# A two-layer vision tower on one core: queries of the first attention by pairs of chunks, its block work at other places, and the second layer's weights and first tokens loaded during the first layer

## The chip, the core and the metric

The kernel runs on 1 core of one Trainium2 chip. The metric is the device time in microseconds (us) of one execution. The engines are PE (TensorE, matrix multiplication), DVE (VectorE), ACT (ScalarE), POOL (GpSimd) and SP (SyncE, which here only issues DMAs). Everything is float32. Each engine takes its instructions in the order in which the program lists them and waits where an operand is not there yet.

## What is computed

An image tower for 128 images: a tokenizer (two convolutions) makes 64 tokens of 256 features for each image. Then come two layers, each one attention and one feed-forward part with experts. Cut to what matters here:

```python
h = tokenizer(x)                                   # (128, 64, 256)
# layer 0, attention over differences: no product of q and k, but relu(q - k)
Q, K, V = (layernorm(h) @ W.T for W in (Wq, Wk, Wv))          # 8 groups of 32 features
attn = einsum("bqkgd,d->bqkg", relu(Q[:, :, None] - K[:, None]), w_mlp) + b_mlp
attn = softmax(relu(attn), axis=2)
h = h + einsum("bqkg,bkdg->bqdg", attn, V)
# layer 0, four experts, each itself a small attention over 64-feature parts of a token
h = h + expert_mixture(layernorm(h))
# layer 1, linear attention: tokens at one position t of all 128 images form a row
h = h + linear_attention(layernorm(h))
# layer 1, eight experts, one for each token (routing by the largest gate, capacity 1280)
h = h + routed_experts(layernorm(h))
```

## The kernel before

The program is one sequence of five stages, and the order on every engine is the order in which the code lists the work (`tc.manual_schedule()`).

**First attention** (`relu_attention`, about 177 to 1080 us). The 128 images form 8 blocks of 16 images. A block's 64 query positions are done 8 at a time: 8 chunks in a block, 64 chunks in all, numbered n; I write j for n modulo 8, the place of a chunk within its block. Relu(q - k) of one chunk has 32 parts (16 pairs i of rows by 2 halves hf of the features). DVE makes 18 of these parts with `larger` (line 530: max(q, k), from which the key is taken off again by a sum made once for a block, `key_sums` and `correction`), POOL 12 with `difference` (line 538, finished by a Relu on ACT, line 539), and ACT alone the remaining 2 with `by_query` (line 548). PE then sums each part over the features with the weights `w_mlp` (`add`, line 340) into the PSUM tile `sc`. When a chunk is summed, the softmax of it is made during the next chunk: `less_max` (DVE, lines 564 to 566), `exponents` (ACT), `sums` (DVE), `weights` (POOL, line 578), `transpose` (PE, line 587), `transposed` (ACT).

A chunk's loop body (lines 703 to 759) is written out by hand. On PE its order is: `add(0,0)`, the place X, `add(8,0)`, `add(4,0)`, the queries of the next chunk (`queries`, line 459: 4 matmuls of 128 columns, which the trace shows as 8 records), the place Y, `add(8,1)`, `add(0,1)`, `add(4,1)`, the seeding of the next `sc` (line 523), the transposes of the last chunk's softmax (line 587), the place Z, `add(12,0)`, `add(12,1)`. On ACT the places O, A, B and C, on DVE V1 (after `less_max`) and V2 (late in the chunk), on POOL W (after `weights`) lie between the steps of the chunk.

The work of a whole block is put at these places by lines 632 to 690: for the next block the statistics and factors of its normalisation (V2, W), the normalised rows (A, B, C), their transposes (X, Z), the keys (`keys`, line 405, four half blocks), the values (`values`, line 424, four quarters), the key sums (Y); for the last block the product with the values (`outcome`, line 480), its transposes (`back`, line 498) and the sum into the stream h2 (`added`, DVE, line 508). Before the change the keys lie at X and Z of j = 4 and 5, the values at X of j = 6, X and Z of j = 7 and Y of the next j = 0; `added` lies once in j = 2, twice in j = 3 and once in j = 4.

The queries' PSUM tile `pc` holds one chunk, in a pool of two; 8 more columns of it take the row maximum of `less_max`.

**Expert attention** (`expert_attention`, to about 1864 us): 64 pairs of images, one after the other, each in a loop body (lines 1268 to 1306) with scores, softmax, product with the values, and `output` (line 1120), which adds the result to h2 in SBUF and after each fourth pair writes these four pairs to DRAM (`hd`, line 1127). The last pair's softmax, its transposes, `mixed` and `output` end the stage. Its softmax weights (`weights`, lines 1087 and 1088) are two POOL operations for each half.

**Linear attention** (`linear_attention`): it reads `hd` back by token position, 4 positions at a time for all 128 images (`Group.load`, line 1365). Before the first matmul it loads its weights on ACT's queue (lines 1335 to 1347), makes some constants on POOL, loads four groups, and runs for group 0: statistics (DVE, lines 1373 and 1374), factors (POOL, 1378 to 1381), normalisation (ACT, 1384), transposes (PE, 1393), queries and keys (PE, line 1421). The constants and small weights of the routing (`Routing.__init__`) are set up just ahead of it, on the same queues.

Routing and the routed experts follow; the change does not touch them.

Of the kernel before, what the change touches and what calls it, by code (L numbers as in the profile page):

```python
# [20 lines left out]
P = 128  # L21
# [269 lines left out]
class Shared:  # L291
# [3 lines left out]
    def __init__(self, c, ctx):  # L295
        def pool(name, bufs, **k):
            return ctx.enter_context(c.tc.tile_pool(name=name, bufs=bufs, **k))

        self.np_, self.bp = pool("an", 2), pool("ab", 2)
        self.atp, self.ep, self.small = pool("aat", 1), pool("ae", 2), pool("as", 1)  # L300
        self.psq = pool("apq", 4, space=PSUM)
# [5 lines left out]
def relu_attention(c, sh, wqkv, wmlp, bmlp, beside):  # L307
# [10 lines left out]
    with (  # L318
# [29 lines left out]
        class Block:  # L348
# [103 lines left out]
            def queries(self, q0):  # L452

                self.pc[q0] = pc = psc.tile([P, 2 * NB * 8 + 8], F32, tag="pc", name="pc")
                pq = pc[:, : 2 * NB * 8].rearrange("p (c i t) -> p c i t", c=2, i=NB)
                xi = self.xT.rearrange("p c n (b t) -> p c (n b) t", b=2)
                for fo in range(2):
                    for fi in range(2):
                        nc.tensor.matmul(  # L459
                            pq[:, fo],  # L460
                            w[:, fi, fo * P : (fo + 1) * P],
                            xi[:, fi, :, q0 : q0 + 8],
# [4 lines left out]
            def queried(self, q0):  # L467
                self.q[q0] = q = ep.tile([P, 2, NB // 2, 8], F32, tag="q", name="q")
                pq = self.pc[q0][:, : 2 * NB * 8].rearrange("p (c i t) -> p c i t", c=2, i=NB)
                nc.scalar.copy(q, pq[:, :, NB // 2 :])  # L470
# [39 lines left out]
        class Chunk:  # L510


            def __init__(self, blk, q0):
                self.blk, self.q0, self.parts, self.m = blk, q0, {}, {}
                self.pc = blk.pc.pop(q0)
                self.pq = self.pc[:, : 2 * NB * 8].rearrange("p (c i t) -> p c i t", c=2, i=NB)
# [43 lines left out]
            def less_max(self):  # L560
                self.e = e = ep.tile([P, 8, T], F32, tag="e", name="e")
                self.mx = mx = ep.tile([P, 8], F32, tag="mx", name="mx")
                pm = self.pc[:, 2 * NB * 8 :]
# [68 lines left out]
        for b, x in enumerate(blocks):  # L632
            n = 8 * b

            if b + 1 < len(blocks):
# [6 lines left out]
                for i in range(4):  # L642
                    at(n + 10 + i // 2, "XY"[i % 2], of(x.back, i))
                    at(n + 10 + (i + 1) // 2, ("V2", "V1")[i % 2], of(x.added, i))
# [15 lines left out]
            else:  # L660
                for i in range(NP):
                    at(n - 21 + i if b > 2 else 1 + i // 4, "V2", of(x.statistics, i))
                at(n - 17 if b > 2 else 2, "W", of(x.factors, 0, 4))
                at(n - 13, "W", of(x.factors, 4, 8))
# [11 lines left out]
            for fo in range(2):  # L676
                at(n - 4 + fo, "X", of(x.keys, 0, fo))
                at(n - 4 + fo, "A", of(x.keyed, 0, fo))
                at(n - 4 + fo, "Z", of(x.keys, 1, fo))
                at(n - 3 + fo, "O", of(x.keyed, 1, fo))  # L680
            at(n - 2, "X", of(x.values, 0))
            at(n - 2, "A", of(x.valued, 0))
            at(n - 2, "Y", x.key_sums)
            at(n - 1, "V1", x.correction)
            at(n - 1, "X", of(x.values, 1))
            at(n - 1, "A", of(x.valued, 1))
            at(n - 1, "Z", of(x.values, 2))
            at(n, "O", of(x.valued, 2))
            at(n, "Y", of(x.values, 3))
            at(n, "B", of(x.valued, 3))  # L690
# [8 lines left out]
        with tc.manual_schedule():  # L699
# [3 lines left out]
            for n in range(len(seq)):  # L703
# [18 lines left out]
                if n + 1 < len(seq):  # L722
                    seq[n + 1][0].queries(seq[n + 1][1])
# [41 lines left out]
def expert_attention(c, sh, hd, normw, wr, br, wqkv, wvT, wproj, bproj, wout):  # L765
# [227 lines left out]
    class Pair:  # L993
# [89 lines left out]
        def weights(self, x):  # L1083
# [3 lines left out]
            nc.gpsimd.tensor_mul(s2, s2, bcast(self.blk.gate[:, self.n, x::2], 1, 8))  # L1087
            nc.gpsimd.tensor_mul(e, e, bcast(sm, 2, T))  # L1088
# [31 lines left out]
        def output(self):  # L1120
# [5 lines left out]
            if p % 4 == 3:  # L1126
                nc.sync.dma_start(
                    hd[2 * p - 6 : 2 * p + 2].rearrange("(n b) t f -> (b t) n f", b=2),
                    h2[:, p - 3 : p + 1],
                )  # L1130

# [82 lines left out]
    def first(cur, new, chunk, last):  # L1214
# [39 lines left out]
        last.added(3)  # L1254
        for k in range(NB):
# [4 lines left out]
    def rest(chunk, last):  # L1260
        with (
# [6 lines left out]
            for p in range(NP):  # L1268
                new = Pair(p + 1, blocks[(p + 1) // NB]) if p + 1 < NP else None
                if p == 0:  # L1270
                    first(cur, new, chunk, last)
                    old, cur = cur, new
                    continue
                do((p, "ACT"))
# [12 lines left out]
                cur.exponents(0)  # L1287
                if new:
# [8 lines left out]
                cur.weights(1)  # L1297
                do((p, "POOL"))
                old.mixed()
                if new:  # L1300
                    for h in range(2):
                        new.values(h)
                        new.values_kept(h)
                old.output()
# [11 lines left out]
def linear_attention(c, hd, hx, out, k, wqk, bqk, wv, bv, wgb):  # L1316
# [7 lines left out]
    NG = 4  # L1324
    with (
        tc.tile_pool(name="lw", bufs=1) as wp,
# [932 lines left out]
```

## Time and profile before

| | us |
|---|---|
| median of 3 runs | 2670.72 (2669.07 to 2671.12) |
| the profiled execution, its own time | 2667.24 |
| span of that execution in the profile | 2665.5 |
| PE busy | 2523.5 (95%) |
| DVE busy | 2009.8 (75%) |
| POOL busy | 1627.9 (61%) |
| ACT busy | 1621.5 (61%) |

The span runs from the first to the last instruction. Busy time is the union of the engine's instructions, averaged over five stages with different limits, so that a share of the whole span says little about one stage. The granted TensorE clock is 0.983 of full speed over the span and 1.00 in the first attention. In the trace a float32 matmul of the code shows as two records.

### The profile page before, as it was taken

To read this page: it belongs to the slowest core of one execution; us is meant where nothing else is said; L and a number is where in the kernel's file an instruction comes from. 1 tells how busy PE (TensorE), PEld (TensorE's weight loads), DVE (VectorE), ACT (ScalarE), POOL (GpSimd) and SP (SyncE) were. 2 spreads that over 40 slices of the span, in tenths; PEclk is the share of its full clock that TensorE was granted. 3 is DMA by queue.
4 is the path that set the end of the run, shared out by engine and by line. 5 is a ranking of instruction groups with operands and counts; after the bars stand their busy time and mean duration, and the time that the engine had idled before them with its cause. 6 is when DMAs were issued, how large, how long until landed. Compare 5 with 4: busy or idle time off the path is not lost.

```text
span 2665.5 us, 81705 instructions
## 1 busy us (share of the span) xinstructions
PE 2523.5 (95%) x35613; PEld 1729.0 (65%) x35613; DVE 2009.8 (75%) x2998; ACT 1621.5 (61%) x3421; POOL 1627.9 (61%) x1426
## 2 busy tenths in 40 slices
PE   8989999999999999899999999998899987999997
PEld 4554444444444444688888888887466565888886
DVE  5759999999999999778787878776467786444443
ACT  2228889898898988666666666665344533232332
POOL 3319999999899999565666665643233313444544
PEclk9999999999999999999999999999899998999998
DMA  3000000000000000000000000000434454555554
GB/s 112 33 13 1 2 1 2 1 2 2 1 2 1 2 13 2 3 20 11 12 19 12 11 20 12 19 12 17 121 73 110 95 127 151 190 183 200 190 186 134
DMA packets 138274, 141.19 MB, mean 53 GB/s; under 512 B 107875, under 2 KB 121701, under 8 KB 130224
## 3 DMA queue, kind: packets, MB, share of 16 engines
q1 hardware_dynamic: 127536, 118.40, 14.7%
q0 software_dynamic: 7648, 14.77, 1.8%
q8 instruction: 281, 4.60, 0.7%
q10 hardware_dynamic: 2720, 2.69, 0.3%
q14 instruction: 89, 0.73, 0.1%
HBM read 104.03 MB, written 32.54 MB: 51 GB/s over the span
## 4 chain that ended last, share of the span: by engine, by line
PE 75%; DVE 13%; issue 5%; ACT 4%; POOL 2%; DMA 1%; SPq 0%; POOLq 0%; DVEq 0%; ACTq 0%
PE sc L340 15%; PE po L2103 6%; PE ph L2087 6%; PE pc L184 5%; PE pt L1097 4%; PE sc L1061 4%; PE pqk L1014 4%; PE pq L1421 4%; PE pv L1036 3%; PE pz L1110 3%; PE pt L587 2%; DVE m L530 2%; PE pc L459 2%; PE pk L405 2%; DVE mx L1073 2%
## 5 line engine op out<-in xcount | busy, mean ns | idle before, releaser
L538 POOL TENSOR_TENSOR m<-q,k 128x1024 f32<-128x1024 f32 x384 | 719.7, 1907 | 56.4 <-PE sc L340 44.5
L530 DVE TENSOR_TENSOR m<-pc,k 128x2048 f32<-128x2048 f32 (+1 forms) x320 | 646.4, 2056 | 0.5 <-ACT q L470 0.5
L340 PE MATMUL sc<-m,wide 128*32 128x512 f32 x4096 | 517.1, 597 | 8.5 <-ACT m L539 6.2
L539 ACT ACTIVATE m<-m 128x1024 f32<-128x1024 f32 x384 | 403.1, 1051 | 21.3 <-POOL m L538 21.3
L340 PEld LDWEIGHTS sc<-m,wide 128*32 128x32 f32 x4096 | 130.9, 109 | 270.1 <-issue 159.4
L548 ACT ACTIVATE m<-k,q 128x64 f32<-128x64 f32 x1024 | 271.1, 340 | 0.9 <-DVE k L417 0.9
L1073 DVE TENSOR_REDUCE mx<-sc 128x16 f32<-128x1024 f32 x128 | 156.0, 1219 | 135.3 <-PE sc L1061 135.3
L1088 POOL TENSOR_TENSOR e<-e,mx 128x1024 f32<-128x1024 f32 x128 | 243.5, 1902 | 10.1 <-POOL mx L1087 0.2
L1020 ACT COPY kr<-pqk 128x512 f32<-128x512 f32 x254 | 137.9, 604 | 142.1 <-PE pqk L1014 142.1
L2087 PE MATMUL ph<-xt,w1s 128*128 128x256 f32 x896 | 198.7, 379 | 3.4 <-DVE xt L2078 2.7
L1087 POOL TENSOR_TENSOR mx<-mx,gate 128x16 f32<-128x16 f32 x128 | 27.6, 216 | 280.3 <-ACT z L1118 150.9
L2103 PE MATMUL po<-w2s,hT 128*128 128x256 f32 x896 | 198.0, 379 | 0.0
L2087 PEld LDWEIGHTS ph<-xt,w1s 128*128 128x128 f32 x896 | 169.9, 190 | 27.9 <-DVE xt L2078 3.4
L2103 PEld LDWEIGHTS po<-w2s,hT 128*128 128x128 f32 x896 | 168.1, 190 | 21.7
L1100 ACT COPY pT<-pt 128x512 f32<-128x512 f32 x256 | 139.0, 600 | 51.6 <-PE pt L1097 51.4
L1074 DVE TENSOR_TENSOR e<-sc,mx 128x1024 f32<-128x1024 f32 x128 | 156.7, 1224 | 4.4
L2121 POOL DMA_INDIRECT out<-y,rout x56 | 56.7, 1013 | 167.8 <-ACT hT L2091 124.8
L1080 DVE TENSOR_REDUCE mx<-e 128x16 f32<-128x1024 f32 x128 | 152.5, 1191 | 4.6 <-ACT e L1077 4.5
L1097 PE MATMUL pt<-ident,e 128*128 128x128 f32 x1024 | 143.0, 282 | 10.0 <-DVE vr L1050 7.3
L2091 ACT ACTIVATE hT<-ph,w1s 128x256 f32<-128x256 f32 x224 | 93.0, 470 | 96.9 <-PE ph L2087 96.9
L2108 ACT ACTIVATE y<-y,gf 128x256 f32<-128x256 f32 x56 | 28.0, 507 | 196.0 <-issue 107.3
L1077 ACT ACTIVATE e<-e 128x1024 f32<-128x1024 f32 x128 | 139.6, 1090 | 1.6 <-DVE e L1074 1.6
(331 smaller groups left out, 5009.6 us busy)
## 6 DMA issues: line engine op xcount, KB each, us to landing
w1s<-in_we SPq DMA_DIRECT2D x30, 1028.0 KB, 5.1
w2s<-in_we SPq DMA_DIRECT2D x30, 1024.0 KB, 4.8
hd<-h SPq DMA_DIRECT2D x16, 512.0 KB, 3.2
x<-hd SPq DMA_DIRECT2D x16, 512.0 KB, 3.6
h<-hd SPq DMA_DIRECT2D x4, 2048.0 KB, 12.7
hx<-h SPq DMA_DIRECT2D x4, 2048.0 KB, 11.7
out<-h SPq DMA_DIRECT2D x4, 2048.0 KB, 20.5
xt<-in_x SPq DMA_DIRECT2D x15, 512.0 KB, 3.5
```

What stands on the lines that cost most here:

```text
L340: nc.tensor.matmul(dst[j : j + 32], wide[:, hf, s : s + 32], part, start=start, stop=stop)
L530: nc.vector.tensor_tensor(m, bcast(self.pq[:, hf, i : i + n], 3, T), k, ALU.max)
L538: nc.gpsimd.tensor_tensor(m, bcast(self.q[:, hf, s : s + 2], 3, T), k, ALU.subtract)
L539: nc.scalar.activation(m, m, AF.Relu)
L548: nc.scalar.activation(self.parts[i, hf][:, q], self.blk.k[:, hf, i], AF.Relu, bias=self.q[:, hf, i - NB // 2, q : q + 1], scale=-1.0,)
L1073: nc.vector.tensor_reduce(mx, sc, AX.X, ALU.max)
L1074: nc.vector.tensor_sub(e, sc, bcast(mx, 2, T))
L1080: nc.vector.tensor_reduce(self.sm[x], self.e[x], AX.X, ALU.add)
L1088: nc.gpsimd.tensor_mul(e, e, bcast(sm, 2, T))
L1097: nc.tensor.transpose(pt[:, cq, :], e[:, i : i + 2, :].rearrange("p e s -> p (e s)"), c.ident)
L2087: nc.tensor.matmul(ph[:, j], self.w1[:, w0 : w0 + P], self.xt[:, fc], start=(fc == 0), stop=(fc == 1))
L2103: nc.tensor.matmul(po, self.hT[:, f, r * P : r * P + P], self.w2[:, f, :], start=(f == 0), stop=(f == 7))
```

## The change

Items 1 and 2 are in the first attention, item 3 is a layout of SBUF that item 4, at the border to the second layer, needs.

1. `queries` makes the queries of two chunks at once: one PSUM tile `pc` holds both, and each matmul has 256 columns instead of 128. The calls come in the chunks j = 0 (for the chunks 2 and 3), j = 3 (4 and 5), j = 5 (6 and 7) and j = 7 (0 and 1 of the next block). The row maximum of `less_max` goes into a part of the chunk's own queries that is no longer needed.
2. The block work lies at other places. Keys: Y and Z of j = 4 and 5, the copies at B and O. Values: Y of j = 2, 4, 6 and 7, copies at B. `added`: twice in j = 2 and twice in j = 3. The factors on POOL: from j = 7 and j = 3 to j = 1 and j = 6.
3. The pools of the tiles `at`, `e`, `q` go to the right side of SBUF, so that they can be closed after the first pair of the expert attention. Their room then holds the new class `Front`.
4. `Front` loads the linear attention's weights at pair 8 of the expert attention on SP's queue, and the first 16 token positions (four groups) as rows of images, one piece each time four pairs have been written, the last two images straight from h2 in SBUF. The last three pairs are written to `hd` in pieces of 2, 1 and 1 pairs. In the last pair `mixed` and `output` of the pair before it come ahead of the softmax sums, three matmuls without use follow them on PE, and the second half's weights are made on DVE. The linear attention starts with seven matmuls without use, normalises group 0 in two halves of two positions, and puts the routing's loads behind group 4's load and its constants into the first head's loop.

```diff
-                self.pc[q0] = pc = psc.tile([P, 2 * NB * 8 + 8], F32, tag="pc", name="pc")
-                pq = pc[:, : 2 * NB * 8].rearrange("p (c i t) -> p c i t", c=2, i=NB)
-                xi = self.xT.rearrange("p c n (b t) -> p c (n b) t", b=2)
+                pc = psc.tile([P, 2, 2, NB, 8], F32, tag="pc", name="pc")
+                for k in range(2):
+                    self.pc[q0 + 8 * k] = pc[:, k]
+                xi = self.xT.rearrange("p c n (b s k t) -> p c s k (n b) t", b=2, k=2, t=8)
                 for fo in range(2):
                     for fi in range(2):
                         nc.tensor.matmul(
-                            pq[:, fo],
+                            pc[:, :, fo],
                             w[:, fi, fo * P : (fo + 1) * P],
-                            xi[:, fi, :, q0 : q0 + 8],
+                            xi[:, fi, q0 // 16],
...
-                pm = self.pc[:, 2 * NB * 8 :]
+                pm = self.pq[:, 0, 0]
...
-                    at(n + 10 + (i + 1) // 2, ("V2", "V1")[i % 2], of(x.added, i))
+                    at(n + 10 + i // 2, ("V1", "V2")[i % 2], of(x.added, i))
...
-                at(n - 17 if b > 2 else 2, "W", of(x.factors, 0, 4))
-                at(n - 13, "W", of(x.factors, 4, 8))
+                at(n - 15 if b > 2 else 2, "W", of(x.factors, 0, 4))
+                at(n - 10, "W", of(x.factors, 4, 8))
...
-                at(n - 4 + fo, "X", of(x.keys, 0, fo))
-                at(n - 4 + fo, "A", of(x.keyed, 0, fo))
+                at(n - 4 + fo, "Y", of(x.keys, 0, fo))
+                at(n - 4 + fo, "B", of(x.keyed, 0, fo))
...
-            at(n - 2, "X", of(x.values, 0))
-            at(n - 2, "A", of(x.valued, 0))
             at(n - 2, "Y", x.key_sums)
             at(n - 1, "V1", x.correction)
-            at(n - 1, "X", of(x.values, 1))
-            at(n - 1, "A", of(x.valued, 1))
-            at(n - 1, "Z", of(x.values, 2))
-            at(n, "O", of(x.valued, 2))
-            at(n, "Y", of(x.values, 3))
-            at(n, "B", of(x.valued, 3))
+            for i, k in enumerate((6 - (b == 1), 4, 2, 1)):
+                at(n - k, "Y", of(x.values, i))
+                at(n - k, "B", of(x.valued, i))
...
-                if n + 1 < len(seq):
-                    seq[n + 1][0].queries(seq[n + 1][1])
+                two = {0: 2, 3: 1, 5: 1, 7: 1}.get(n % 8)
+                if two and n + two < len(seq):
+                    x, q0 = seq[n + two]
+                    x.queries(q0)
...
+            if p == NP - 1:
+                front.rows(B - 2, B)
+            n = {NP - 3: 2, NP - 2: 1, NP - 1: 1}.get(p, 4 * (p % 4 == 3))
+            if n:
                 nc.sync.dma_start(
-                    hd[2 * p - 6 : 2 * p + 2].rearrange("(n b) t f -> (b t) n f", b=2),
-                    h2[:, p - 3 : p + 1],
+                    hd[2 * (p - n + 1) : 2 * p + 2].rearrange("(n b) t f -> (b t) n f", b=2),
+                    h2[:, p - n + 1 : p + 1],
                 )
+            if p == NP - 3:
+                front.rows(B - 16, B - 8)
+            elif p == NP - 2:
+                front.rows(B - 8, B - 2)
+            elif n == 4 and p > 3:
+                front.rows(2 * p - 14, 2 * p - 6)
...
+                if p == 8:
+                    front.weights()
...
                 cur.exponents(0)
+                if not new:
+                    old.mixed()
+                    old.output()
+                    c.busy(ps([P, 2 * D], "idle"), wt.w, 3)
...
-                cur.weights(1)
+                cur.weights(1, nc.gpsimd if new else nc.vector)
...
+    def rows(self, b0, b1):
+        nc, NG = self.c.nc, self.NG
+        n = 4 * NG
+        x = self.x.rearrange("p g t f -> p (g t) f")
+        if b1 < B:
+            nc.sync.dma_start(x[b0:b1], self.hd[b0:b1, 0:n, :])
+            return
+        for b in range(2):
+            nc.sync.dma_start(x[b0 + b : b0 + b + 1], self.c.h2[b * T : b * T + n, B // 2 - 1, :])
...
         with tc.manual_schedule():
+            c.busy(psp.tile([P, 2 * D], F32, tag="pp", name="idle"), w[:, 0], 7)
             for g in range(4):
-                groups[g].load()
+                groups[g].x = front.group(g)
             for g in range(3):
                 for i in range(NG):
                     groups[g].statistics(i)
-                groups[g].factors()
+                    if g == 0 and i % 2:
+                        groups[0].factors(i - 1, i + 1)
+                        for j in range(i - 1, i + 1):
+                            groups[0].normal(j)
                 if g == 0:
-                    for i in range(NG):
-                        groups[0].normal(i)
                     groups[0].transpose()
+                else:
+                    groups[g].factors()
             groups[4].load()
+            routing.load()
...
+        at(0, 9, routing.constants)
+        at(0, 10, lambda: routing.weights_sum(psp.tile([P, 2 * D], F32, tag="pp", name="pw")[:, 0:E]))
```

## The prediction, made before the changed kernel had run

> **What bounds the kernel now.** I read the page first, then the windows of one steady block of the first attention (chunks 24 to 31), then the timeline of a chunk, and last the timeline at the border of the layers.
>
> ```profile
> PE 2523.5 (95%) x35613; PEld 1729.0 (65%) x35613; DVE 2009.8 (75%) x2998; ACT 1621.5 (61%) x3421; POOL 1627.9 (61%) x1426
> PE 75%; DVE 13%; issue 5%; ACT 4%; POOL 2%; DMA 1%; SPq 0%; POOLq 0%; DVEq 0%; ACTq 0%
> ```
>
> The chain that ends last is PE for three quarters. The change can pay where PE is too late, or where nobody works. The eight chunks of a block, in order j = 0 to 7 (stretch, its length, then busy time of PE, weight loads, DVE, ACT, POOL):
>
> ```profile
> 533.60:546.80 13.20, 13.20 (x132) 6.21 (x128) 12.72 (x12) 11.96 (x28) 12.29 (x8) 1.00 0.01 1
> 546.80:560.00 13.20, 13.20 (x372) 6.66 (x368) 12.77 (x13) 11.81 (x28) 12.32 (x8) 1.00 0.02 4
> 560.00:573.60 13.60, 13.38 (x128) 5.74 (x124) 13.29 (x13) 13.24 (x33) 12.20 (x8) 1.00 0.01 2
> 573.60:587.70 14.10, 14.10 (x132) 5.98 (x124) 13.87 (x15) 12.21 (x29) 13.09 (x11) 1.00 0.00 1
> 587.70:602.10 14.40, 14.40 (x118) 5.49 (x120) 13.32 (x15) 13.49 (x33) 13.11 (x9) 1.00 0.00 1
> 602.10:616.40 14.30, 14.30 (x124) 6.12 (x120) 12.71 (x13) 12.40 (x29) 12.24 (x8) 1.00 0.01 2
> 616.40:629.20 12.80, 12.80 (x160) 6.37 (x156) 12.59 (x12) 10.53 (x24) 12.28 (x8) 1.00 0.00 1
> 629.20:643.70 14.50, 14.50 (x132) 7.27 (x128) 12.96 (x15) 13.27 (x34) 13.84 (x12) 1.00 0.01 2
> ```
>
> PE looks full everywhere, but that is the modelled end of a matmul. DVE is nearly as full: 104.2 of 110.1 us. So two limits alternate: DVE binds where its busy time is within 0.3 us of the length (j = 2, 3, 6), PE where DVE has a gap of 0.4 to 1.6 us. What PE needs I took from the timeline, from a group's start to the next group's start:
>
> ```profile
> 602.76 1.98 PE L405 MATMUL pk<-xT,w 128*128 128x512 f32 x4
> 606.53 1.16 PE L459 MATMUL pc<-xT,w 128*128 128x128 f32 x8
> 617.08 1.99 PE L424 MATMUL pv<-w,xT 128*128 128x256 f32 x8
> ```
>
> Half a block of keys holds PE 1.91 us, the queries of a chunk 1.09, a quarter of the values 1.92 (1.82 right behind other full matmuls). In the same way: the 32 sums of a chunk 7.0, seeding 0.97, softmax transposes 1.08, half an outcome 1.41, four transposes 0.55 to 0.59, key sums 0.5. At the border:
>
> ```profile
> 1857.14 1.97 PE L1097 MATMUL pt<-ident,e 128*128 128x128 f32 x8 [0.19 <-POOL e L1088]
> 1863.30 0.42 DVE L1125 TENSOR_TENSOR h<-h,po 128x256 f32<-128x256 f32 x1 [8.50 <-PE po L1124]
> 1863.75 0.36 SPq L1127 DMA_DIRECT2D hd<-h  x1
> ...
> 1874.73 0.43 DVE L1373 BATCH_NORM_STATS2 st<-x 128x6 f32<-128x256 f32 x1 [0.68 <-DMA x<-hd]
> ...
> 1879.08 2.07 ACT L1384 ACTIVATE x<-x,nb,rs 128x256 f32<-128x256 f32 x4 [17.00 <-DVE mv L1374]
> ...
> 1882.36 7.88 PE L1421 MATMUL pq<-w,xT 128*128 128x512 f32 x16
> ```
>
> From the end of the last addition (1863.72) to the first product of the second layer (1882.36) PE has nothing of use for 18.64 us: 2.9 for the write to DRAM, about 1 of restart, 7.0 for the read back, 7.6 for statistics, factors, normalisation and transposes.
>
> **What the Trainium skill says.** "TensorE: Matmul & The Clock Gate", section "LDWEIGHTS (loading the stationary operand)": a weight load takes the time of its columns, whatever its number of rows. The trace agrees: 8 loads for the queries take 0.97 us, 0.12 each, as much as their 128 columns of data, so that 256 columns behind one load use it better. The same page, "What's actually happening": after an idle window of about 3.4 us the array runs at half clock until it has been busy as long. The trace fits: the 8 transposes of the last pair take 1.97 us, those inside the loop 1.09. "DMA: Bandwidth & Descriptors", section "Latency and other measured facts", speaks of a fixed cost of about 2 us for one DMA; here the write of 512 KB lands 2.9 us after its issue, so a small copy can't land much before 2.
>
> **The change, part by part.**
>
> *Queries by two.* Removed: eight times 1.09 a block. Added: four times 1.92 (8 records of 128 columns by 256, the form of the values' row). On PE 8.7 - 7.7 = 1.0 us less a block.
>
> *Keys and values at Y.* Nothing is added or removed, but a stretch of full matmuls that stands alone costs about 0.2 us more than one behind another (1.92 against 1.82, and the split of the sums), and four X places fall away: 0.1 to 0.2 each. With that, PE's need by chunk (sums, seeding, transposes 9.05, plus block work) is, before: 13.1, 13.0, 11.9, 11.9, 14.0, 14.0, 12.6, 14.0. After: j = 0 12.2; j = 1 11.9; j = 2 12.6 (values come in); j = 3 12.6; j = 4 14.6 (9.05 + keys 1.91 + values 1.82 + keys 1.91 - 0.1); j = 5 14.6 (9.05 + queries 1.92 + keys 1.8 + 1.9); j = 6 11.4; j = 7 12.6.
>
> *Additions.* Each `added` costs DVE 0.6 (0.68 busy, overlapped). One moves from j = 4 to j = 2. DVE's need with its small gaps (the busy column plus 0.25) becomes: 12.95, 12.95, 14.25, 14.1, 12.9, 12.95, 12.85, 13.15.
>
> The time of a chunk is the larger need, with 0.1 for PE-bound ones: 12.95 + 12.95 + 14.25 + 14.1 + 14.7 + 14.7 + 12.85 + 13.15 = 109.65 against 110.1. Gains are in j = 7 (14.5 to 13.15) and 0 and 1 (0.25 each), losses in j = 2, 4 and 5. So almost all that PE gains is stopped by DVE. I take 0.5 to 1.0 a block, since the 0.25 is generous where DVE is ahead: 5.5 for seven blocks. The first query call lies on the path and becomes 0.85 longer (chunk 0 was made in 0.89); net 5. Bounds: a loss of 6, if each of j = 4 and 5 also costs the 0.4 below, and a gain of 15, if DVE's own sum were nearly reached.
>
> *What waits with it.* The key and value copies move on ACT from A to B; an ACT that is there before PE has done Y stands with `by_query` and the Relus behind it, and PE waits for these. In j = 4 ACT reaches B some 5.0 us after the chunk's last sum (5.65 at 607.72 less the copies that left), values are ready at 5.7: 0.4 to 0.7 late, against a wait of 0.76 that ACT has anyway later in this chunk (before the `transposed` copy). I cost it at nothing.
>
> *Factors on POOL.* 1.7 us (four operations) more in j = 1 and 6 instead of 3 and 7. POOL stands 0.8 to 2.0 us for PE in most chunks, which hides most; the rest is caught up in the longer j = 2 and 7. Nothing. *Pools moved to the right side*: no instruction.
>
> *Last pair.* The second half's weights on DVE: about 0.2 + 1.22 instead of 0.22 + 1.90 on POOL behind the first half. But the sums now stand behind `added` of pair 62, which waits for its product (about 1852.3 instead of sums from 1851.15): some 1.5 late. The two cancel (1857.1 either way). The three unused matmuls keep the clock: transposes 1.09 for 1.97, `mixed` 2.1 for 2.56. Gain 0.7; between -0.8 and +1.5.
>
> *First tokens.* All rows but the last two images' are in SBUF before the end (96 KB follow the write of pair 62, nine us ahead). After the last addition two copies of 16 KB from h2: two issues of 0.36 on SP and 2.0 to 2.9 to land, so the statistics begin 2.5 to 3.3 after the addition instead of 11.0. From there: two positions' statistics 1.1, factors 1.9 on POOL, twice in a row (the second pair's end 5.0 after landing), normalisation 1.1, last transpose and copy 1.2: 7.2 to 7.4 against 7.6. The first product comes at +10.3 instead of +18.64: gain 8.3; between 7.5 and 9. SP has the last write to hd behind the two copies, then group 4, which waits for the transposes of group 0 as before. The seven unused matmuls (7 x 0.86 = 6 us) end before the transposes.
>
> *Weights and constants.* Seven DMAs on an SP queue that has one write in four pairs, five memsets of 0.2 on POOL at pair 8: hidden by POOL's idle time, 0 to 0.5. The routing's weight sum, hidden in the gap before, now lies between products: +0.5.
>
> Sum: -5 - 0.7 - 8.3 + 0.5 = -13.5. On the profiled execution: 2667.2 - 13.5 = 2653.7. That execution was 3.5 us below the median, so the median becomes 2670.7 - 13.5 = 2657.
>
> **The rivals.**
>
> *DVE takes it all*: the attention stays as it is, the border pays 9.0 less 0.5 and the 0.85 of the first queries: 2663. For it: DVE's 104.2 of 110.1. Against: j = 7 and 0 are clearly PE's.
>
> *The stalls go too*: PE's and DVE's limits no longer alternate, and a block nears DVE's sum plus its gaps, 106: seven times 4, and 8.5: 2634 to 2642, say 2638. Against it: `less_max` waits for the last sum of each chunk, so that neither engine can run more than a part of a chunk ahead.
>
> *Tokens don't come early*: SP works in order, the last rows wait for the write of pair 62, and a copy into a single partition may be slow. If the statistics start as before, 5 + 0.7 remain: 2665.
>
> *Slower*: the full stretch of 3.7 us at Y in j = 4, 5 and 7, with the copies at B. If ACT stands there for the whole last step (1.9) and only its 0.76 of slack hides it, each of the three chunks grows by about 1.2: 3.6 x 7 = 25 us, the 5 are not won, the border gives 8.5 back: 2687. It decides once ACT's wait at B exceeds some 0.8 us in these chunks.
>
> **How the numbers follow.** Forecast 2657 with 0.54, DVE takes it all 0.22, stalls gone 0.08, tokens late 0.08, slower 0.08. The range from 2645 to 2668 holds the forecast with its bounds and two rivals, and leaves out the far gain and the far loss. What a measurement can tell from no change is 0.2%, 5.3 us: faster means below 2665.4. Of the forecast nearly all is below, of the DVE case three quarters, of the late tokens half, all of the far gain: 0.81. Slower than 2676 is the last case and a rest, 0.08; 0.11 lies between.
>
> **What would show it.** In the changed profile a steady block near 109 to 109.6, with j = 4 and 5 at 14.7 and j = 7 near 13.1, DVE at 104 as before; the queries' rows 8 records of 128x256 in about 2.0; from the last addition to the first product about 10 us; the last transposes near 1.1. It is wrong if ACT's key or value copies show waits over 0.8 us, if j = 4 or 5 pass 15, or if the statistics of group 0 begin more than 4 us after the last addition.

## The result, and the profile after

The changed kernel takes 2805.66 us (median; 2797.19 to 2808.93), the kernel before, run beside it, 2669.89. The ratio is 1.0508, with a 95% interval from 1.0493 to 1.0523: 5% slower, 136 us, where 2657 had been forecast. The profiled execution has a span of 2806.1 us against 2665.5.

From the page of the changed kernel, the engines and then five groups (busy time, mean of one in ns, idle time of the engine ahead of them, and what ended most of it):

```profile
PE 2576.6 (92%) x35377; PEld 1720.8 (61%) x35377; DVE 2017.0 (72%) x3000; ACT 1625.6 (58%) x3421; POOL 1628.5 (58%) x1428
...
L540 POOL TENSOR_TENSOR m<-q,k 128x1024 f32<-128x1024 f32 x384 | 720.1, 1907 | 74.6 <-PE sc L342 60.4
L532 DVE TENSOR_TENSOR m<-pc,k 128x2048 f32<-128x2048 f32 (+1 forms) x320 | 646.8, 2057 | 124.1 <-ACT q L473 124.1
L342 PE MATMUL sc<-m,wide 128*32 128x512 f32 x4096 | 552.8, 616 | 106.6 <-DVE m L532 96.3
L541 ACT ACTIVATE m<-m 128x1024 f32<-128x1024 f32 x384 | 399.9, 1049 | 109.8 <-POOL m L540 109.8
...
L581 POOL TENSOR_TENSOR e<-e,mx 128x512 f32<-128x512 f32 x64 | 66.9, 1045 | 149.5 <-DVE mx L578 119.8
```

Three of these groups on the page of the kernel before, where their lines have other numbers:

```profile
L530 DVE TENSOR_TENSOR m<-pc,k 128x2048 f32<-128x2048 f32 (+1 forms) x320 | 646.4, 2056 | 0.5 <-ACT q L470 0.5
L340 PE MATMUL sc<-m,wide 128*32 128x512 f32 x4096 | 517.1, 597 | 8.5 <-ACT m L539 6.2
L539 ACT ACTIVATE m<-m 128x1024 f32<-128x1024 f32 x384 | 403.1, 1051 | 21.3 <-POOL m L538 21.3
```

The busy times of DVE, POOL and ACT are nearly those of before (DVE 2017.0 against 2009.8). PE's is 53 us longer, but it has 236 instructions fewer; its sums took longer one by one (616 ns on average, 597 before). So no work has been added. The new thing is on the right. `larger` on DVE had 0.5 us of idle time ahead of it and now has 124.1, all ended by line 473, ACT's copy of the queries (`queried`). The sums on PE wait 106.6 instead of 8.5, the Relus on ACT 109.8 instead of 21.3, the weights on POOL 149.5 instead of 21.9. The timeline below shows how the one stall is handed on to these. The list of waits (total, times, longest) counts it:

```profile
PEld sc L342 <- DVE m L532: 167.3, 96, 2.8
...
DVE m L532 <- ACT q L473: 124.1, 32, 4.7
POOL e L581 <- DVE mx L578: 119.8, 37, 6.6
```

DVE waits 32 times, once in every second chunk, 3.9 us on average.

To place it I measured each chunk from the start of one row maximum (`less_max`) to the next. Chunks 24 to 31 of the changed kernel, j = 0 to 7 (stretch, length, then busy time and instructions of PE, weight loads, DVE, ACT, POOL, then the granted clock):

```profile
585.20:603.07 17.87, 14.53 (x159) 5.58 (x153) 12.82 (x12) 13.38 (x33) 13.19 (x8) 1.00 0.00 1
603.07:616.03 12.96, 12.90 (x358) 6.38 (x337) 12.74 (x13) 11.04 (x25) 11.62 (x11) 1.00 0.02 4
616.03:634.38 18.35, 15.31 (x134) 6.05 (x128) 14.01 (x14) 14.83 (x35) 14.80 (x10) 1.00 0.00 1
634.38:648.43 14.05, 13.88 (x124) 5.98 (x124) 13.84 (x14) 12.16 (x29) 12.08 (x7) 1.00 0.01 1
648.43:666.01 17.58, 14.99 (x116) 5.69 (x116) 12.81 (x13) 12.89 (x30) 11.28 (x8) 1.00 0.00 1
666.01:680.73 14.72, 14.72 (x124) 6.26 (x120) 12.72 (x12) 12.44 (x29) 12.26 (x8) 1.00 0.01 2
680.73:699.15 18.42, 15.08 (x152) 6.47 (x148) 12.82 (x13) 10.73 (x24) 13.97 (x12) 0.81 0.00 1
699.15:713.19 14.04, 13.76 (x124) 6.20 (x120) 12.91 (x13) 11.77 (x27) 12.29 (x8) 1.00 0.01 2
```

The even chunks take 17.6 to 18.4 us, where before they took 12.8 to 14.4; the odd ones are at 12.96 to 14.72. DVE's busy time in the even ones is what it was, but for the `added` that moved from j = 4 to j = 2. The last chunk's clock is an average; the last section comes back to it. From the first row maximum to the last the stage takes 1010.3 us instead of 864.6: 145.7 more, while everything else together takes 5.1 less.

Inside one even chunk (j = 4; start, length, engine and line, and in brackets the idle time ahead of it and who ended it):

```profile
648.43 0.69 DVE L567 TENSOR_REDUCE pc<-sc 128x8 f32<-128x512 f32 x1
...
649.42 0.69 DVE L569 SCALAR_TENSOR_TENSOR e<-sc,mx 128x512 f32<-128x512 f32 x1
...
650.15 0.63 ACT L574 ACTIVATE e<-e 128x512 f32<-128x512 f32 x1 [1.26 <-DVE e L569]
650.68 1.05 ACT L550 ACTIVATE m<-k,q 128x64 f32<-128x64 f32 x4
...
651.64 1.99 ACT L541 ACTIVATE m<-m 128x1024 f32<-128x1024 f32 x2
...
653.53 0.24 ACT L473 COPY q<-pc 128x128 f32<-128x128 f32 x1
...
653.81 2.29 DVE L532 TENSOR_TENSOR m<-pc,k 128x2048 f32<-128x2048 f32 x1 [3.69 <-ACT q L473]
...
656.02 0.68 DVE L577 TENSOR_REDUCE mx<-e 128x8 f32<-128x512 f32 x1
...
656.15 1.06 PE L342 MATMUL sc<-m,wide 128*32 128x512 f32 x8 [0.67 <-DVE m L532]
...
657.10 1.04 POOL L581 TENSOR_TENSOR e<-e,mx 128x512 f32<-128x512 f32 x1 [4.83 <-ACT m L541]
...
659.14 1.06 PE L342 MATMUL sc<-m,wide 128*32 128x512 f32 x8 [1.92 <-DVE m L532]
...
660.04 1.06 ACT L541 ACTIVATE m<-m 128x1024 f32<-128x1024 f32 x1 [2.06 <-POOL m L540]
```

After the row maximum and the exponent's argument (until 650.1) DVE's next instruction is `larger(0,4,1)`. It reads this chunk's columns of the query tile and the keys, and both have long been there. It starts only at 653.81, just after ACT has copied out the queries of the *other* chunk of the pair (653.53 + 0.24). ACT gets to that copy late, since the exponentials, a `by_query` step of four instructions and two Relus stand before it in its queue. From there the stall runs on: DVE's softmax sums come late, so POOL stands 4.83 before the weights (the bracket names ACT, but over the program the list of waits puts most of this on DVE's sums, 119.8), so POOL's next differences and ACT's Relus are late (2.06), and PE waits for DVE's parts (0.67 and 1.92). Before, the same two instructions lay side by side:

```profile
648.32 3.37 DVE L530 TENSOR_TENSOR m<-pc,k 128x2048 f32<-128x2048 f32 x2
...
649.27 0.24 ACT L470 COPY q<-pc 128x128 f32<-128x128 f32 x1
```

There the copy (for the next chunk) ran in the middle of two of DVE's maxima. It read another PSUM tile, since each chunk had its own. Over the whole trace, 63 of the 64 copies overlapped one of DVE's maxima in time. In the changed kernel 31 of the 32 copies from the next pair's tile still do, but none of the 32 from the tile that DVE is reading.

So the change made a wait that no line of it names: two chunks' queries lie in one PSUM tile (512 columns), DVE reads one half, ACT the other, and DVE's read is ordered behind ACT's. The order stands in the program as built: in the trace `larger(0,4,1)` waits on ACT's semaphore in all 32 even chunks and in no odd one, and in none of the 64 chunks before the change. The Trainium skill, "PSUM — Partial Sum Buffer", section "PSUM bank collisions raise a hardware error ⚠️", says that two engines must not be in one bank and quadrant at once, and that the compiler's scheduler "adds a dependency between any two instructions on different engines that touch the same bank × 32-partition quadrant, reads and writes alike". The trace agrees that two reads by two engines were ordered, in 32 waits of up to 4.7 us. Whether this rule or the sharing of the tile as such put the order into the program, the runs can't separate.

The border of the layers, in the changed kernel:

```profile
2008.34 1.09 PE L1098 MATMUL pt<-ident,e 128*128 128x128 f32 x8 [0.20 <-DVE e L1089]
...
2013.64 0.42 DVE L1126 TENSOR_TENSOR h<-h,po 128x256 f32<-128x256 f32 x1 [5.36 <-PE po L1125]
2014.09 1.25 SPq L1389 DMA_DIRECT2D x<-h  x2
...
2017.08 0.43 DVE L1429 BATCH_NORM_STATS2 st<-x 128x6 f32<-128x256 f32 x1 [3.02 <-DMA x<-h]
...
2019.98 1.09 ACT L1441 ACTIVATE x<-x,nb,rs 128x256 f32<-128x256 f32 x2 [7.56 <-POOL nb L1438]
...
2023.68 7.13 PE L1478 MATMUL pq<-w,xT 128*128 128x512 f32 x16 [0.24 <-ACT xT L1451]
```

This part of the trace went as forecast: the statistics start 3.0 us after the last addition, and the first product of the second layer 9.6 us after its end (2023.68 less 2014.06), instead of 18.64. The last transposes take 1.09 instead of 1.97.

### The profile page after: what moved, and what is told of

Its sections match the earlier page's. It is cut to its first block, busy times and chain, and to the rows that moved or that the text cites. A ratio compares the mean times of both kernels' runs of the same rounds, so it can differ in the third digit from the quotient of the medians.

```text
span 2806.1 us, 81274 instructions
## 1 busy us (share of the span) xinstructions
PE 2576.6 (92%) x35377; PEld 1720.8 (61%) x35377; DVE 2017.0 (72%) x3000; ACT 1625.6 (58%) x3421; POOL 1628.5 (58%) x1428
## 3 DMA queue, kind: packets, MB, share of 16 engines
q1 hardware_dynamic: 128684, 119.48, 14.4%
## 5 line engine op out<-in xcount | busy, mean ns | idle before, releaser
L532 DVE TENSOR_TENSOR m<-pc,k 128x2048 f32<-128x2048 f32 (+1 forms) x320 | 646.8, 2057 | 124.1 <-ACT q L473 124.1
L342 PE MATMUL sc<-m,wide 128*32 128x512 f32 x4096 | 552.8, 616 | 106.6 <-DVE m L532 96.3
L541 ACT ACTIVATE m<-m 128x1024 f32<-128x1024 f32 x384 | 399.9, 1049 | 109.8 <-POOL m L540 109.8
L581 POOL TENSOR_TENSOR e<-e,mx 128x512 f32<-128x512 f32 x64 | 66.9, 1045 | 149.5 <-DVE mx L578 119.8
```

What stands on the lines that cost most here:

```text
L342: nc.tensor.matmul(dst[j : j + 32], wide[:, hf, s : s + 32], part, start=start, stop=stop)
L532: nc.vector.tensor_tensor(m, bcast(self.pq[:, hf, i : i + n], 3, T), k, ALU.max)
L541: nc.scalar.activation(m, m, AF.Relu)
```

## The experiments

Three explanations stood. *The shared tile*: DVE waits behind ACT's late copy from the pair's tile. *The places*: keys and values at Y are full stretches, with ACT's copies late. *The clock*: over the first attention the granted clock is 0.96 in the changed kernel and was 1.00. Twelve kernels were run, each compared with the kernel before on the same chip (2664.5 to 2668.0 there; 2669.89 for the changed kernel). Since the chips differ a little, the ratios are what can be compared from row to row.

| kernel | us | ratio to before, 95% | first attention, us |
|---|---|---|---|
| changed | 2805.66 | 1.0493 to 1.0523 | 1010.3 |
| e1: changed, queries one chunk at a time | 2665.55 | 0.9988 to 1.0006 | 870.6 |
| e2: before, queries by two alone | 2825.07 | one execution | 1023.3 |
| e3: changed, both copies before the pair | 2667.29 | 0.9995 to 1.0012 | 871.1 |
| e4: before, new places alone | 2672.46 | 1.0006 to 1.0026 | 870.6 |
| e5: before, border alone | 2659.53 | 0.9969 to 0.9984 | 864.6 |
| e6: e3 with the old places | 2671.25 | 1.0005 to 1.0024 | 875.3 |
| e7: changed, odd copies on DVE | 2668.31 | 0.9999 to 1.0014 | 872.8 |
| e8: e5, one quarter of the values earlier | 2657.50 | 0.9959 to 0.9979 | 864.0 |
| e9: e8 and keys earlier | 2657.36 | 0.9963 to 0.9987 | 864.4 |
| e10: e8 and a second quarter earlier | 2657.64 | 0.9956 to 0.9979 | 863.2 |
| e11: e6 with keys and values spread | 2662.48 | 0.9968 to 0.9986 | 870.9 |
| e12: changed, copy sooner on ACT | 2672.53 | 1.0021 to 1.0045 | 876.1 |

The last column is the time from the first row maximum to the last in the profiled execution; before it is 864.6.

**e1, the pairs undone.** Each chunk gets its own tile again; the rest of the change stays.

```diff
-                pc = psc.tile([P, 2, 2, NB, 8], F32, tag="pc", name="pc")
+                self.pc[q0] = pc = psc.tile([P, 2 * NB * 8 + 8], F32, tag="pc", name="pc")
...
-                two = {0: 2, 3: 1, 5: 1, 7: 1}.get(n % 8)
-                if two and n + two < len(seq):
-                    x, q0 = seq[n + two]
-                    x.queries(q0)
+                if n + 1 < len(seq):
+                    seq[n + 1][0].queries(seq[n + 1][1])
```

> The changed kernel with one part undone: queries are formed one chunk at a time again, each chunk in a PSUM tile of its own; the new block work, the early weights and the early token rows stay. Theory (the wait on the shared tile: in an even chunk VectorE's next maximum, which reads the pair's query tile, is ordered behind ScalarE's copy of the neighbour chunk's queries out of the same tile): the whole loss goes, 2650 to 2665 us, idle of VectorE's maxima behind ScalarE's query copy under 5 us in all, even chunks back near 13 to 14.7 us. Rival one (keys and values at the new places are full stretches, with ScalarE's copies late): still above 2690 us, the long chunks stay at j = 4, 5, 7. Rival two (the granted clock in the attention is lower with the new work): above 2690 us, all chunks longer alike.

The loss is gone, 2665.55 us (half a us past the end of what was expected), DVE's wait back at 0.5 us. What I had not expected is that j = 2 and j = 4 stay long, at 14.91 and 15.47 (the windows of these two chunks):

```profile
674.44:689.35 14.91, 14.69 (x136) 6.77 (x132) 13.92 (x14) 13.90 (x34) 13.43 (x9) 1.00 0.01 1
703.40:718.87 15.47, 15.47 (x124) 6.79 (x124) 12.71 (x14) 12.80 (x30) 11.32 (x8) 1.00 0.00 1
```

**e2, the pairs alone.** The opposite edit: in the kernel before, the diff's first two hunks and the call by `two`, nothing else.

> The kernel before with one part alone: queries by two chunks in one PSUM tile, with the old block work and the old loads. Theory (the wait on the shared tile): nearly the whole loss comes with it, 2800 to 2825 us (32 even chunks by 4 to 5 us = 128 to 160 us on 2670), VectorE's maxima idle about 120 us behind ScalarE's query copy, even chunks long and odd ones as before. Rival one (the new places of keys and values): 2665 to 2680 us, since these are not in it. Rival two (granted clock): 2665 to 2690 us.

2825.07 us, from a single execution, so without an interval; 159 us above the kernel before are far beyond the few us by which executions differ here. The edit brings the whole loss without any of the new places, in the same wait (a group of its page):

```profile
L529 DVE TENSOR_TENSOR m<-pc,k 128x2048 f32<-128x2048 f32 (+1 forms) x320 | 646.7, 2057 | 128.5 <-ACT q L470 128.5
```

So the new places fall as the cause of the loss. The clock is 0.96 in this stage too, so that it comes with the stall; this run alone doesn't clear it. The table of chunks does: j = 0, 2 and 4 of the changed kernel have a clock of 1.00 and are 3.2 to 4.7 us longer than before all the same.

**e3, the tile shared, the copies early.** ACT copies both chunks' queries in the odd chunk before the pair begins.

```diff
-                self.q[q0] = q = ep.tile([P, 2, NB // 2, 8], F32, tag="q", name="q")
+                self.q[q0] = q = ep.tile([P, 2, NB // 2, 8], F32, tag="q", name="q", bufs=3)
...
-                    seq[n + 1][0].queried(seq[n + 1][1])
+                    for x, q0 in seq[n + 1 : n + 3] if n % 2 else ():
+                        x.queried(q0)
```

To make room for the third copy, `kb` has one buffer and a constant fewer columns.

> The changed kernel with queries by two chunks kept, but ScalarE copies the queries of both chunks of a pair out of the tile in the odd chunk before the pair begins, so that no copy from the tile is left while VectorE reads it in the even chunk (three copies of queries are kept instead of two). Theory (the wait on the shared tile): the wait goes though the tile is still shared, 2648 to 2668 us, VectorE's maxima idle under 10 us behind ScalarE's query copy. Rival one (the new places of keys and values): above 2690 us. Rival two (the matmul over both chunks itself, through its lateness or the shared tile's late release): above 2750 us, the even chunks still 4 us longer.

2667.29 us. The timeline of the same chunk j = 4, with the copies ten us ahead:

```profile
694.62 0.41 ACT L473 COPY q<-pc 128x128 f32<-128x128 f32 x2
...
703.06 0.69 DVE L567 TENSOR_REDUCE pc<-sc 128x8 f32<-128x512 f32 x1
...
704.05 0.69 DVE L569 SCALAR_TENSOR_TENSOR e<-sc,mx 128x512 f32<-128x512 f32 x1
...
704.66 2.28 DVE L532 TENSOR_TENSOR m<-pc,k 128x2048 f32<-128x2048 f32 x1
...
706.86 0.67 DVE L577 TENSOR_REDUCE mx<-e 128x8 f32<-128x512 f32 x1
```

`larger` follows the exponent's argument at once (704.66; in the changed kernel it stood 3.69 us). So the tile may be shared, and the matmul over two chunks doesn't make this loss by itself. The clock is back at 1.00.

**e7, the same copy on the other engine.**

```diff
-                nc.scalar.copy(q, self.pc[q0][:, :, NB // 2 :])
+                copy = nc.vector.tensor_copy if q0 % 16 else nc.scalar.copy
+                copy(q, self.pc[q0][:, :, NB // 2 :])
```

> The changed kernel with one edit: the copy of the odd chunk's queries out of the pair's tile is made by VectorE instead of ScalarE, at the same place of the order. The tile is shared as before and is copied as late as before. Theory (VectorE's read of the tile is ordered behind ScalarE's read of it, and ScalarE comes late): with both reads on one engine the wait is gone, VectorE pays 32 copies of some 0.25 us more, 2664 to 2678 us. Rival (the late time of the copy, or the shared tile as such, whoever copies): still above 2750 us.

2668.31 us; the wait is gone (timeline, j = 4):

```profile
595.84 0.69 DVE L570 SCALAR_TENSOR_TENSOR e<-sc,mx 128x512 f32<-128x512 f32 x1
...
596.45 0.28 DVE L474 COPY q<-pc 128x128 f32<-128x128 f32 x1
...
596.65 2.28 DVE L533 TENSOR_TENSOR m<-pc,k 128x2048 f32<-128x2048 f32 x1
```

My text was wrong on one point: at the same place in the order, DVE reaches the copy sooner than ACT did, at once after 595.84, so the copy is not as late as before. The run shows that 0.28 us of DVE's time is cheaper than the wait for ACT; it doesn't part "another engine" from "late".

**e12, the same engine, sooner.** This run does. ACT still makes the copy, in the even chunk, from the shared tile, but ahead of the exponentials:

```diff
                 ch.add(4, 0)
+                if n % 2 == 0:
+                    seq[n + 1][0].queried(seq[n + 1][1])
                 if old:
                     old.less_max()
...
                 if n + 1 < len(seq):
-                    seq[n + 1][0].queried(seq[n + 1][1])
+                    if n % 2:
+                        seq[n + 1][0].queried(seq[n + 1][1])
```

> The changed kernel with one line moved: in an even chunk ScalarE copies the other chunk's queries out of the pair's tile before the exponentials of that chunk (where ScalarE stands idle 1.26 us in the changed kernel), not behind them and five further instructions. Tile, engines and number of copies as in the changed kernel. Theory (the loss is VectorE's wait for a copy that comes late in ScalarE's order): the wait falls from 3.7 to 4.7 us to under 0.5 a chunk and the loss goes, 2662 to 2672 us. Rival (any two engines reading the pair's tile in one chunk cost the time): above 2750 us.

```profile
705.62 0.69 DVE L567 TENSOR_REDUCE pc<-sc 128x8 f32<-128x512 f32 x1
705.98 0.25 ACT L473 COPY q<-pc 128x128 f32<-128x128 f32 x1
...
706.61 0.69 DVE L569 SCALAR_TENSOR_TENSOR e<-sc,mx 128x512 f32<-128x512 f32 x1
...
707.22 2.28 DVE L532 TENSOR_TENSOR m<-pc,k 128x2048 f32<-128x2048 f32 x1
707.34 0.63 ACT L574 ACTIVATE e<-e 128x512 f32<-128x512 f32 x1 [1.10 <-DVE e L569]
```

2672.53 us, just past the end of what was expected. ACT copies at 705.98, while DVE is at the row maximum, and `larger` starts without delay. Over the program 6.1 us of this wait remain, in 14 chunks, up to 1.3 us each, where under 0.5 had been expected. `larger` still waits on ACT's semaphore in all 32 even chunks; it only comes in time. The cost therefore is the lateness of the copy in ACT's order: one line moved takes the loss from 5.1% to 0.3%, which is 127 of the 136 us.

**e4, the new places alone.** In the kernel before, only the diff's hunks for factors, keys, values and `added`, which begin so:

```diff
-                    at(n + 10 + (i + 1) // 2, ("V2", "V1")[i % 2], of(x.added, i))
+                    at(n + 10 + i // 2, ("V1", "V2")[i % 2], of(x.added, i))
...
```

> The kernel before with one part alone: the new places of the block work (statistics' factors, keys, values, additions to the token rows), queries one chunk at a time, no early weights or rows. Theory (the wait on the shared tile): this part is innocent, 2662 to 2672 us, within 0.3% of before. Rival one (the new places of keys and values): 2690 us or more, chunks at j = 4, 5 and 7 over 15 us.

2672.46 us (0.5 past the end of what was expected), 4.3 us by the ratio (1.6 to 6.9). So the places do cost a little, about a sixth of the 25 us that the slower rival had for them. By chunk (mean of five for each place, the chunks 9 to 48) j = 2 goes from 13.66 to 14.91 and j = 4 from 14.39 to 15.37, j = 7 from 14.42 to 13.37: 111.12 a block against 110.28.

**e5, the border alone.** The early loads and the new last pair only. Against the changed kernel this is e1's edit and the old places put back, for the values among others:

```diff
-            for i, k in enumerate((6 - (b == 1), 4, 2, 1)):
-                at(n - k, "Y", of(x.values, i))
-                at(n - k, "B", of(x.valued, i))
...
```

> The kernel before with one part alone: the early weights, the early token rows and the new last pair of the expert attention (items 3 and 4 of the change); queries one chunk at a time and the old block work. My step for this part was 8.3 + 0.7 - 0.5 = 8.5 us: 2656 to 2660 us on 2666.3. If the border's gain is partly lost elsewhere: the difference of the two kernels with the new block work so far, 6.9 us, gives 2659.5. If the gain of the tokens were not real: 2664 to 2667.

2659.53 against 2666.01: 6 us by the ratio (4.3 to 8.3), the first attention as before (864.6). The gain is there, a little under my 8.5. The trace of the changed kernel shows the products of the second layer starting 9 us sooner; where the rest of that goes was not looked into.

**e6, e8 to e11: does the table of needs hold, and is there a better kernel?** In e6, e3 got the old places, by e5's edit. In the others, work of PE went to chunks where, by the table, DVE leaves room. e8 is the first of these hunks on e5, e10 both; e9 adds the third to e8; e11 is e6 with the second, with the first at `n - 6` and the third as `n - 5 + fo`:

```diff
-            at(n - 2, "X", of(x.values, 0))
-            at(n - 2, "A", of(x.valued, 0))
+            at(n - 5, "X", of(x.values, 0))
+            at(n - 5, "A", of(x.valued, 0))
...
-            at(n - 1, "X", of(x.values, 1))
-            at(n - 1, "A", of(x.valued, 1))
+            at(n - 2, "X", of(x.values, 1))
+            at(n - 2, "A", of(x.valued, 1))
...
-                at(n - 4 + fo, "X", of(x.keys, 0, fo))
-                at(n - 4 + fo, "A", of(x.keyed, 0, fo))
+                at(n - 6 + 2 * fo, "X", of(x.keys, 0, fo))
+                at(n - 6 + 2 * fo, "A", of(x.keyed, 0, fo))
```

> Queries by two chunks, both copies made in the odd chunk before the pair, the early loads and the last pair as in the changed kernel, but the old places of the block work. By my chunk table (needs of PE with the pair's 1.92 in j = 0, 3, 5, 7 and of VectorE) the chunks would be 14.0, 12.95, 13.55, 14.1, 13.6, 14.9, 12.85, 14.9 = 110.85 a block against 110.1 before: about 5 us more than the border part alone, 2664 us. If queries by two pay what my step said (1.0 us a block of PE's time, on the path): 2653 us.

> As the border part alone, and in the old block work the first quarter of a block's values is formed in the third chunk before (j = 3, where PE has 2 us of room against VectorE) instead of the second (j = 6 to j = 3; PE is then freer at j = 6). By my chunk table j = 6 is bound by VectorE at 12.85 either way and j = 3 stays at 14.15, so within 2 us of the border part alone: a control of the table.

> As the run before it, and the first half of the first keys goes from j = 4 to j = 2, the second half from j = 5 to j = 4. By my chunk table j = 5 falls from 14.3 to about 13 (VectorE's own need), j = 4 stays, j = 2 grows by 0.3: about 1.0 us a block, 7 us less than the border part alone, some 2651 us. If ScalarE (13.2 us busy of 13.7 at j = 2, plus a copy of 0.6) stops it, no gain or up to 5 us more.

> Queries one chunk at a time, the border part, and two quarters of the values moved: the first from j = 6 to j = 3, the second from j = 7 to j = 6. By my chunk table j = 7 falls from 14.3 to about 13.2 and nothing else changes: 7 to 8 us less than the run with one quarter moved, some 2650 us. If j = 7 is not bound by PE, no gain: 2657 us.

> As the run with queries by two, early copies and the old places, and PE's work spread where VectorE leaves room: the first quarter of the values at j = 2, the second at j = 6, the first half of the first keys at j = 3 and the second at j = 4. By my chunk table 14.0, 12.95, 13.55, 14.6, 13.6, 13.1, 12.85, 13.2 = 107.85 a block: 21 us less than the run with the old places (3.0 us by seven blocks), some 2643 us. If ScalarE stops it at j = 2 and 3 (its copies come on top of 13.2 us busy), 2650 us. If the table is wrong on what binds, 2660 us or more.

e6 came to 2671.25, worse than 2664: with the old places queries by two don't pay either, they cost (875.3 us for the stage against e5's 864.6). Against e5 the chunks j = 0 and 5, into which a call for two chunks falls, grow from 13.24 to 14.05 and from 14.32 to 14.97. e8, the control, came out 2.0 us below e5. e9, e10 and e11 missed by 6, 8 and 19 us: e9 and e10 ended at the "no gain" of their texts, e11 at its "2660 us or more" for a wrong table. Relieved of 1.9 us of PE's work, j = 7 of e10 fell by 0.3 against e8 (14.32 to 13.99), not to 13.2; j = 5 of e9 fell by 0.5, to 13.84 and not to 13, and j = 2, which took the work, grew by as much. So something besides PE and DVE holds a chunk. In j = 7 of e10 the waits name POOL's differences and ACT's Relus on them:

```profile
PEld sc L342 <- ACT m L542: 2.0, 3, 1.4
ACT m L542 <- POOL m L541: 1.7, 1, 1.7
```

That reading is argued from the waits; no run tested it. e8 and e10 are faster than the kernel before by 0.2 to 0.4%, but their intervals overlap that of e5, so that the border is the only part of the change whose gain is shown.

## Why the prediction was wrong

**The step that failed** is *Queries by two*: "Removed: eight times 1.09 a block. Added: four times 1.92 [...] On PE 8.7 - 7.7 = 1.0 us less a block." It priced the matmuls, and these came out as said (1.99 us for 8 records of 128x256). It did not price the buffer: I never asked who else reads the tile once it holds two chunks. The term that was left out is 32 even chunks by about 4.4 us (chunks 9 to 48, j = 0, 2, 4, 6 in the changed kernel less e3: 5.3, 4.7, 3.4, 4.3), 141 us, against 139.2 between the two stages. The experiments for this are e2 (the wait comes with this step alone) and e1, e3, e7 and e12 (it goes when the tile, the time of the copy or its engine is changed). No rival held it: the slower one put the stall at Y, into ACT's key and value copies, and e4 gives the new places 4 us, not 25.

**The gain of that step** isn't there even without the wait. e3 and e1 differ by this step and by the earlier copies with their third buffer, and their stages take 871.1 and 870.6 us. With the old places it costs some 11 us (e6 against e5). "DVE takes it all" had the gain at nothing; that DVE is what takes it is not shown. One reading was loose, too: the 0.12 us for a weight load is the distance from one load to the next in a row of eight that overlap; a load's own record is 0.19 us long (line 459, before).

**Keys and values at Y, additions**: with the wait removed (e3) the chunks are 13.26, 13.09, 14.23, 14.15, 14.47, 14.72, 13.18, 13.98, where 12.95, 12.95, 14.25, 14.1, 14.7, 14.7, 12.85, 13.15 had been forecast. Seven are within 0.35; j = 7 is 0.8 over. The sum is 111.07 instead of 109.65, so that the forecast gain of 5 us is a loss of about 6. With the queries one chunk at a time (e1, e4) j = 4 is at 15.37, past the 15 that the prediction named as a sign of being wrong. "The time of a chunk is the larger need" of PE and DVE is the rule that fails here, and again in e9, e10 and e11.

**What waits with it, "nothing"**: ACT's value copy waits 1.29 us in j = 7 of e3, past the 0.8 that I had named as the point of decision. That chunk is the one that is 0.8 over its forecast; whether by this wait was not tested.

**Last pair and first tokens**: 0.7 and 8.3 forecast. The first product comes at +9.6 instead of +10.3; the whole part is worth 4.3 to 8.3 us in time. *Factors on POOL*, *pools* and *weights and constants* were not run alone; in e5, which holds the last two, no loss shows.

Without the wait (e1, e3, e7) the whole change gives 2666 to 2668 us. That looks like the upper end of my range, but the kernel before took 2666 there, not the 2670.7 from which I had counted: the ratios are 0.9997 to 1.0006, no gain. So the forecast 13.5 us would not have come without the wait either: the new places spend most of the border's gain.

## What to carry to other kernels

When two pieces of work are put into one PSUM tile, list every engine that reads or writes the tile and when, and treat two readers on different engines as ordered. If one of them is far back in its own queue, the other stands still for as long. Before giving up such a tile, move the late reader forward or to the other reader's engine; here one moved line was worth 127 us. A saving on one engine should be costed twice: once in that engine's time, and once as the waits that the new buffer layout makes for the others.

## What the runs showed of the hardware

Two reads at different columns of one PSUM tile, by ACT and DVE, never ran at the same time in the changed kernel (0 of 32, against 63 of 64 with separate tiles). This is the order of the program as built; what the chip would do without it, no run shows.

The granted TensorE clock was lower in just the two kernels with the stall: 0.96 over the first attention in the changed kernel and in e2, against 1.00 before and in all the others. The trace's records of it hold nothing but full and half clock. In this stage of the changed kernel 19 stretches are at half clock, each 3.41 or 6.83 us long, 85 us in all, and every one lies in even chunks. The 0.81 of the chunk from 680.73 to 699.15 us is such a stretch, 690.54 to 697.37, averaged with the full clock of the rest. PE is busy less in this stage (902.75 of 1010.3 us, against 856.5 of 864.6 before). Whether its gaps cause the half clock was not tried.

It is a small part of the loss. Among the even chunks 10 to 62, 16 have such a stretch and 11 have none; those with one are longer than those of the same place j without by 1.0 us on average. That makes the clock's part an estimated 16 us or so of the 141. The five chunks at j = 4 without one are at 17.58 us each, where e3 has 14.47 for this place.
